# Graph attention with residual and layer norm: the queries' order read back earlier, the residual's bias summed on VectorE, the norm in single steps, q, k and v further ahead

## The chip, the cores and the metric

The kernel runs on one core of a Trainium2 chip, all in float32. The metric is the device time of one execution in microseconds. An engine is named as in the profile: PE is TensorE, DVE is VectorE, ACT is ScalarE, POOL is GpSimd (which also issues the gathers and scatters through DMA), SP is the queue that issues the plain DMAs. The five run side by side, each its own list of instructions in order, and wait for one another at semaphores.

## The reference

Sixteen graphs (b) of 1024 nodes (n) with 512 numbers each (d), 8 heads of 64; one adjacency matrix `adj` of 1024 x 1024 for all.

```python
q = (x @ Wq + bq).reshape(b, n, H, HD)          # k and v alike
scores = jnp.einsum('bqhd,bkhd->bhqk', q, k) / jnp.sqrt(jnp.float32(HD))
scores = scores + (1.0 - adj)[None, None, :, :] * -1000000000.0
attn = jax.nn.softmax(scores, axis=-1)
out = jnp.einsum('bhqk,bkhd->bqhd', attn, v).reshape(b, n, d)
return _layernorm(x + out @ Wo + bo)
```

The matrix is sparse and uneven: the first nodes have many neighbours, most have a few.

## The kernel before, in words

**Sparse attention by gathering.** The queries are sorted by their number of neighbours (`ranks`): eight tiles of 128 queries each. For tile t the kernel keeps lists (`edges`) of `OWN[t]` neighbours per query and, for the two tiles of the highest degree, `BLOCKS[t]` blocks of 128 further (query, neighbour) pairs. One block is 128 such pairs, one per partition: 29 own and 6 further ones, so 35 blocks in a batch and 560 in all. For a block POOL gathers rows of k and v (L809, tile kvg) and, once per tile or per further block, rows of q (L793 qt, L803 qg); DVE multiplies q by k (L826) and sums over each head (L830); ACT takes exponentials (L840); v is weighed by ACT (L850) or DVE (L854, `by_act` says which); own blocks are summed on DVE (L866), further ones with a matmul (L875, L876).

**The steps.** The loop over n at the end of the kernel writes the program out in one order for all engines: step n belongs to block n, with look-ahead (gathers 8 blocks ahead, products 4, exponentials 3). 34 steps of negative n lead in. `later(k, fn)` puts work k steps on into the middle of a step, `later_last` at its end. The simple jobs of the start (`loads`, `ranks`, `bias_setup`, `checks`, one `edges` per tile) are generators that run on to their next `yield` once a step; `EDGES_FROM[t]` is the step at which the lists of tile t begin. A list begins with a gather of 128 rows of `adj` in the sorted order (L412); three steps later the row is multiplied by the places 1 to 1024 (L417), and then DVE takes the eight largest at a time (L424, MAX8) and clears them (L426): ten rounds for the last tile, two for the one before, one for the others.

**The order of the queries.** `ranks` reads `adj` (8 tiles), sums its rows on ACT (L359), makes keys, turns them with PE (L369), counts on DVE how many keys are smaller (L376, eight passes over 1024), and scatters the queries to their places in DRAM with eight indirect DMAs of POOL (L384); SP reads the list back (L390) and DVE makes integers of it (L392, `asked_row`). No list, gather of q or store of a result can be issued before.

**q, k and v.** `pair(b, j)` makes q, k and v of two tiles of x with TensorE (L545, L661, with seven products of a fast 2x2 scheme for k and v); DVE and ACT take the sums out of PSUM, SP writes them to DRAM (`q_rows`, `kv_rows`, three batches in a ring). These units of TensorE work (`fronts`) run batches ahead of the attention. When all eight tiles of a batch are sent, a matmul makes the mean of v for queries without neighbours (L605) and SP writes it as the last row (L610); with that the batch counts as `set_up`, and DVE reduces its norms (L614). Gathers of a batch are issued only when it is set up.

**Which TensorE work in which step.** Each step gives TensorE a `share` in units (0.86 for a product of 128 x 512, 1.72 for two, 0.44 for four transposes); products of the output come first, then fronts. In the lead-in the share is 3.45. At the start of each batch it is set so that at its end the fronts are a fixed number of batches on (`goal`: the number of the batch plus 2, plus `EARLY / 35`). When the fronts have run out, some 50 steps before the end, ten attention tiles that were set aside in DRAM before (`SPILL`, the tiles 102 to 111) are finished beside the last ones, and the gathers go 11 ahead.

**The end of a tile.** When all blocks of a tile are in, it is normalised (L884 to L893), turned by PE (L901), and waits in `done`. `load_y` gathers the rows of x for the residual on POOL (L720); while there are fronts, and else for every odd t, POOL adds the bias `bo` to them two or three steps later (L726). `finish` makes the product with Wo, and DVE adds it to y and sums the row (L744; without POOL's bias L743 and L744). Then the norm: the mean in the next step (L749), squares on ACT at the end of the same step (L753), variance and its power -1/2 two steps on (L756 on DVE, L757 on POOL), the shift three steps on (L760), the result at the end of the fourth (L763), and the store two steps behind that, an indirect DMA of POOL (L767).

Of the kernel before, what the change touches and what calls it, by code (L numbers as in the profile page):

```python
# [14 lines left out]
OP = mybir.AluOpType  # L15
# [13 lines left out]
AHEAD = 8  # L29
KG_BUFS, QG_BUFS, QT_BUFS, PV_BUFS, Y_BUFS = 8, 4, 4, 5, 5  # L30
NO_ROW = 65536.0
# [6 lines left out]
ROWS = 3  # L38
EARLY = 11
LEAD_IN = 34  # L40
EDGES_FROM = (-14, -13, -12, -10, -8, -4, -6, -15)

# [110 lines left out]
def kernel(  # L153
# [66 lines left out]
    with ExitStack() as main:  # L220
# [125 lines left out]
        def ranks():  # L346
            for _ in range(2):
# [22 lines left out]
            yield  # L370
# [3 lines left out]
            yield  # L374
            for t in range(NT):
                nc.vector.scalar_tensor_tensor(  # L376
                    keys, row, key[:, t:t + 1], place, op0=OP.is_lt, op1=OP.min, accum_out=rank[:, t:t + 1]
                )
                if t % 3 == 2:
                    yield  # L380
            nc.vector.tensor_copy(rank_row, rank)
            yield
            for t in range(NT):
                nc.gpsimd.indirect_dma_start(  # L384
                    out=order_views[t], out_offset=bass.IndirectOffsetOnAxis(ap=rank_row[:, t:t + 1], axis=0),
                    in_=asked[:, t, :], in_offset=None,
                )
            for _ in range(2):
                yield
            nc.sync.dma_start(ranked, order.rearrange("(t p) c -> p t c", p=P))  # L390
            yield
            nc.vector.tensor_copy(asked_row, ranked[:, :, 0])  # L392
# [15 lines left out]
        def edges(t):  # L408
# [302 lines left out]

        loaded, biased = {}, {}

        def load_y(b, t, k=None):
            if k is None:
                Y[b, t] = work.tile([P, D], F32, tag="y", name=f"y_{b}_{t}", bufs=Y_BUFS)
            else:
                Y[b, t] = work.tile([P, 2, D], F32, tag=f"t{k % 4 + 1}", name=f"y_{b}_{t}", bufs=1)[:, 0, :]
            loaded[b, t] = now[0]
            nc.gpsimd.indirect_dma_start(  # L720
                out=Y[b, t], out_offset=None, in_=x_rows,
                in_offset=bass.IndirectOffsetOnAxis(ap=asked_row[:, t:t + 1], axis=0), element_offset=b * N * D,
            )

            if fronts or t % 2:
                later(2 if fronts else 3, lambda: nc.gpsimd.tensor_tensor(Y[b, t], Y[b, t], bo_bc, op=OP.add))  # L726
                biased[b, t] = True

# [6 lines left out]
        def finish(b, t):  # L735

            def out(p):
# [3 lines left out]
                st = small.tile([P, 5], F32, name="stats", bufs=6)  # L741
                if (b, t) not in biased:
                    nc.vector.tensor_tensor(y, p, y, op=OP.add)  # L743
                nc.vector.scalar_tensor_tensor(  # L744
                    y, p if (b, t) in biased else bo_bc, 1.0, y, op0=OP.mult, op1=OP.add, accum_out=st[:, 0:1]
                )

# [7 lines left out]
                def variance():  # L755
                    nc.vector.tensor_scalar(st[:, 2:3], st[:, 2:3], 1.0 / D, EPS, op0=OP.mult, op1=OP.add)  # L756
                    nc.gpsimd.tensor_tensor(st[:, 3:4], st[:, 2:3], neg_half, op=OP.pow)  # L757

# [28 lines left out]
        def gather(n):  # L787
            b, t, i = blocks[n]
            assert t in listed
            if i == 0:  # L790
                tag, bufs = ("qt", QT_BUFS) if fronts or t % 2 else ("x", 3)
                QT[b, t] = work.tile([P, D], F32, tag=tag, name=f"qt_{b}_{t}", bufs=bufs)
# [6 lines left out]
            else:  # L799
                g = first[t] + i - OWN[t]  # L800
                tag, bufs = ("qg", QG_BUFS) if fronts or i % 2 else ("xT", 4)
                QG[n] = work.tile([P, D], F32, tag=tag, name=f"qg_{n}", bufs=bufs)
# [39 lines left out]
        def by_act(n):  # L842
            b, t, i = blocks[n]
            return 0 < i < OWN[t] or n % 2 == 0

# [117 lines left out]
        prep.setdefault(12 - LEAD_IN, []).append(bias_setup())  # L963
        prep.setdefault(-24, []).append(checks())
        preps = [loads(), ranks()]
        prep.setdefault((B - 1) * NB - 4, []).append(guard())
        with tc.manual_schedule():
# [13 lines left out]
            while n < total or plan or rest or urgent or done or finishing or spilled:  # L981
# [105 lines left out]
```

## Time and profile before

| | |
|---|---|
| median of 3 runs | 2124.21 us (2122.94 to 2130.22) |
| the profiled execution | 2142.24 us |
| its span, first to last instruction | 2140.5 us |
| mean granted TensorE clock | 0.967 |
| busy: PE, DVE, ACT, POOL | 1946.7, 1810.1, 1686.2, 1474.0 us |

A row of a group names line, engine, operation, tiles (out<-in) and shapes, then the total busy time and the mean in ns of one, then the idle time of the engine before them and what ended it. A row of waits reads: engine, the instruction that waited, what it waited for, total us, number, longest. A row of the timeline: start, duration in us, engine, line. A row of windows: the stretch, its length, then busy us and instructions per engine, the granted TensorE clock, the busy share and the rate of the DMAs. "issue" is time in which an engine waited for nothing that the profile shows.

### The profile page before, as it was taken

How to read it: one execution, taken by the hardware profiler on the slowest of the kernel's cores; microseconds unless marked ns; L12 is line 12 of the kernel's file. 1: busy time of each engine (PE TensorE's matmuls, PEld its weight loads, DVE VectorE, ACT ScalarE, POOL GpSimd, SP SyncE). 2: the span in 40 equal slices, each digit the busy share in tenths (PEclk: the TensorE clock that was granted, in tenths of full speed). 3: DMA queues.
4: the chain of work that ended last, by engine and by line, in shares of the span. 5: the costliest groups of instructions: out<-in, count | busy, mean ns of one | idle time of the engine just before them, and what ended most of it. 6: DMA issues, size and time to landing. Idle time of an engine off the chain costs nothing. (4 is left out here: it accounts for less than half of the span.)

```text
span 2140.5 us, 26366 instructions
## 1 busy us (share of the span) xinstructions
PE 1946.7 (91%) x5334; PEld 930.5 (43%) x5334; DVE 1810.1 (85%) x3545; ACT 1686.2 (79%) x7024; POOL 1474.0 (69%) x1350
## 2 busy tenths in 40 slices
PE   8968999999999999999999999999999999998664
PEld 4423454444444444444444444444444444443222
DVE  2699999888988988798888878898889899997675
ACT  5526999788887988698797878888887889897575
POOL 1453778787776867667686766777677774668884
PEclk9988999999999999999999999999999999999887
DMA  6455888878787787878787786888878698978773
GB/s 251 133 182 182 276 277 282 298 252 293 237 283 241 266 305 240 281 230 283 257 280 277 246 279 203 285 282 268 293 241 308 223 317 306 318 229 305 220 233 107
DMA packets 183656, 549.49 MB, mean 257 GB/s; under 512 B 30879, under 2 KB 30907, under 8 KB 183486
## 3 DMA queue, kind: packets, MB, share of 16 engines
q0 software_dynamic: 121632, 403.22, 58.0%
q1 hardware_dynamic: 59248, 139.53, 17.4%
q10 hardware_dynamic: 2606, 4.99, 0.7%
q14 instruction: 126, 1.03, 0.1%
q8 instruction: 44, 0.72, 0.1%
HBM read 435.44 MB, written 136.89 MB: 267 GB/s over the span
## 5 line engine op out<-in xcount | busy, mean ns | idle before, releaser
L850 ACT ACTIVATE pv<-kvg,pv 128x64 f32<-128x64 f32 x3584 | 902.7, 339 | 1.6 <-remote 1.6
L809 POOL DMA_INDIRECT kvg<-kv_rows,key_row x560 | 638.0, 1139 | 306.5 <-issue 107.4
L545 PE MATMUL pq<-wq,xT 128*128 128x512 f32 x1024 | 483.3, 604 | 12.8 <-DVE q L572 11.2
L545 PE MATMUL po<-wo,oT 128*128 128x512 f32 x944 | 436.5, 602 | 6.3 <-ACT oT L905 3.4
L826 DVE TENSOR_TENSOR qk<-qt,kvg 128x512 f32<-128x512 f32 x464 | 355.6, 766 | 52.4 <-DMA kvg<-kv_rows,key_row 43.7
L830 DVE TENSOR_REDUCE s<-qk 128x8 f32<-128x512 f32 x560 | 380.7, 680 | 6.5
L545 PEld LDWEIGHTS pq<-wq,xT 128*128 128x128 f32 x1024 | 194.6, 194 | 244.8 <-issue 216.5
L545 PEld LDWEIGHTS po<-wo,oT 128*128 128x128 f32 x944 | 180.8, 194 | 227.6 <-issue 209.4
L840 ACT ACTIVATE pv<-s,absent 128x8 f32<-128x8 f32 x464 | 135.5, 293 | 150.5 <-DVE s L830 88.1
L661 PE MATMUL x<-b,xT 128*128 128x512 f32 x504 | 242.0, 603 | 3.3 <-ACT e L674 3.3
L866 DVE TENSOR_TENSOR pv<-pv,pv 128x520 f32<-128x520 f32 x336 | 242.6, 722 | 0.1
L661 PE MATMUL pp<-t,s 128*128 128x512 f32 x504 | 238.3, 595 | 1.1 <-DVE s L531 1.0
L753 ACT ACTIVATE ysq<-y,stats 128x512 f32<-128x512 f32 x128 | 91.9, 718 | 113.9 <-DVE stats L749 107.9
L726 POOL TENSOR_TENSOR y<-y,bo_bc 128x512 f32<-128x512 f32 x118 | 158.7, 1345 | 24.2 <-DMA y<-in_x_dram,asked_row 21.6
L793 POOL DMA_INDIRECT qt<-q_rows,asked_row x128 | 144.7, 1130 | 35.9 <-issue 35.0
L767 POOL DMA_INDIRECT out_dram<-y,asked_row x128 | 144.8, 1132 | 34.7 <-issue 22.1
L720 POOL DMA_INDIRECT y<-in_x_dram,asked_row x128 | 143.2, 1118 | 32.0 <-issue 31.7
L557 ACT ACTIVATE sq<-q 128x128 f32<-128x128 f32 x512 | 150.7, 299 | 13.7 <-DVE q L572 13.4
L757 POOL TENSOR_TENSOR stats<-stats,neg_half 128x1 f32<-128x1 f32 x128 | 83.4, 652 | 101.2 <-DVE stats L756 78.4
L557 ACT ACTIVATE sq<-kv 128x128 f32<-128x128 f32 x512 | 150.6, 299 | 0.0
L661 PEld LDWEIGHTS x<-b,xT 128*128 128x128 f32 x504 | 96.0, 193 | 118.7 <-issue 109.1
L661 PEld LDWEIGHTS pp<-t,s 128*128 128x128 f32 x504 | 95.0, 192 | 110.3 <-issue 101.9
(170 smaller groups left out, 2928.8 us busy)
## 6 DMA issues: line engine op xcount, KB each, us to landing
kv_rows<-kv SPq DMA_DIRECT2D x128, 512.0 KB
x<-in_x_dram SPq DMA_DIRECT2D x128, 256.0 KB
q_rows<-q SPq DMA_DIRECT2D x128, 256.0 KB
kvg<-kv_rows,key_row POOLq DMA_INDIRECT x560
adj<-in_adj_dram POOLq DMA_DIRECT2D x8, 512.0 KB
spill<-oT SPq DMA_DIRECT2D x10, 256.0 KB
oTs<-spill SPq DMA_DIRECT2D x10, 256.0 KB
qt<-q_rows,asked_row POOLq DMA_INDIRECT x128
```

The costliest lines, as they stand in the source:

```text
L545: nc.tensor.matmul(p, lhs()[:, ts(c, P)], w[:, c, :], start=(c == 0), stop=(c == NPAIR - 1))
L557: nc.scalar.activation(sq, s[:, ts(h, P)], AF.Square, accum_out=NRM[b][:, i, t, h:h + 1])
L661: nc.tensor.matmul(R[bank], l[:, ts(c, P)], right[:, c, :], start=(first and c == 0), stop=(c == 1), skip_group_check=True,)
L720: nc.gpsimd.indirect_dma_start(out=Y[b, t], out_offset=None, in_=x_rows, in_offset=bass.IndirectOffsetOnAxis(ap=asked_row[:, t:t + 1], axi ...
L726: later(2 if fronts else 3, lambda: nc.gpsimd.tensor_tensor(Y[b, t], Y[b, t], bo_bc, op=OP.add))
L767: nc.gpsimd.indirect_dma_start(out=out_rows[b, t], out_offset=bass.IndirectOffsetOnAxis(ap=asked_row[:, t:t + 1], axis=0), in_=y, in_offse ...
L793: nc.gpsimd.indirect_dma_start(out=QT[b, t], out_offset=None, in_=q_rows[b % ROWS], in_offset=bass.IndirectOffsetOnAxis(ap=asked_row[:, t: ...
L809: nc.gpsimd.indirect_dma_start(out=KG[n], out_offset=None, in_=kv_rows[b % ROWS], in_offset=bass.IndirectOffsetOnAxis(ap=key_row[:, g:g + ...
L826: nc.vector.tensor_tensor(QK[n], q, KG[n][:, 0:D], op=OP.mult)
L830: nc.vector.tensor_reduce(S[n], QK.pop(n).rearrange("p (h d) -> p h d", d=HD), axis=AX.X, op=OP.add)
L850: nc.scalar.activation(pv[:, ts(h, HD)], v[:, ds(D + h * HD, HD)], AF.Copy, scale=pv[:, D + h:D + h + 1])
L866: nc.vector.tensor_tensor(PV[b, t], PV[b, t], pv, op=OP.add)
```

## The change

Four things change, and some buffers with them.

1. *The order sooner.* `ranks` yields less often: the sums of three rows of `adj` per step instead of two, no step of its own for keys and copies, and each scatter is issued as soon as its rank is there, not all eight behind the last. The first use of the order moves from step -15 to step -20. `EDGES_FROM` begins most lists three steps sooner. The multiplication by place goes from POOL to DVE, and in the first 17 steps ACT alone weighs v.
2. *The bias on VectorE.* `load_y` no longer adds the bias; every tile takes the two instructions L743 and L744 that only few took. A product with Wo begins a step later after the load, five tiles of y may be loaded instead of four, and y has six buffers.
3. *The norm in steps.* Mean 1, squares 2, variance 3, power 4, shift 5, result 6 steps on; the store follows two steps behind as it did.
4. *q, k and v further ahead.* `EARLY` is 13 instead of 11, and in the goal of the first batch `FIRST`, 9, comes on top. The gathered q tiles of both kinds share seven buffers in place of four and four.

```diff
-KG_BUFS, QG_BUFS, QT_BUFS, PV_BUFS, Y_BUFS = 8, 4, 4, 5, 5
+KG_BUFS, Q_BUFS, PV_BUFS, Y_BUFS = 8, 7, 5, 6
-EARLY = 11
+EARLY = 13
+FIRST = 9
-EDGES_FROM = (-14, -13, -12, -10, -8, -4, -6, -15)
+EDGES_FROM = (-17, -16, -15, -13, -11, -8, -7, -18)
...
                 nc.scalar.activation(ADJ[t], ADJ[t], AF.Copy, accum_out=asked[:, t, 1:2])
-                if t % 2:
+                if t % 3 == 2:
                     yield
...
+                if t:
+                    nc.vector.tensor_copy(rank_row[:, t - 1:t], rank[:, t - 1:t])
+                    scatter(t - 1)
                 if t % 3 == 2:
                     yield
-            nc.vector.tensor_copy(rank_row, rank)
-            yield
-            for t in range(NT):
-                nc.gpsimd.indirect_dma_start(
...
-            nc.gpsimd.tensor_tensor(v, v, place, op=OP.mult)
+            nc.vector.tensor_tensor(v, v, place, op=OP.mult)
...
-            if fronts or t % 2:
-                later(2 if fronts else 3, lambda: nc.gpsimd.tensor_tensor(Y[b, t], Y[b, t], bo_bc, op=OP.add))
-                biased[b, t] = True
...
-                if (b, t) not in biased:
-                    nc.vector.tensor_tensor(y, p, y, op=OP.add)
-                nc.vector.scalar_tensor_tensor(
-                    y, p if (b, t) in biased else bo_bc, 1.0, y, op0=OP.mult, op1=OP.add, accum_out=st[:, 0:1]
-                )
+                nc.vector.tensor_tensor(y, p, y, op=OP.add)
+                nc.vector.scalar_tensor_tensor(y, bo_bc, 1.0, y, op0=OP.mult, op1=OP.add, accum_out=st[:, 0:1])
...
-                later_last(1, spread)
-                later(2, variance)
-                later(3, shift)
-                later_last(4, norm_out)
+                later_last(2, spread)
+                later(3, variance)
+                later(4, power)
+                later(5, shift)
+                later_last(6, norm_out)
...
-            return 0 < i < OWN[t] or n % 2 == 0
+            return 0 < i < OWN[t] or n % 2 == 0 or n < NB // 2
...
-        prep.setdefault(-24, []).append(checks())
+        prep.setdefault(-22, []).append(checks())
...
-                    goal = fronts_time - (n // NB + 2 + EARLY / NB) * batch_time
+                    goal = fronts_time - (n // NB + 2 + (EARLY + (FIRST if n < NB else 0)) / NB) * batch_time
...
-                    if tile_done not in loaded and sum(b * NT + t not in SPILL for b, t in Y) < 4:
+                    if tile_done not in loaded and sum(b * NT + t not in SPILL for b, t in Y) < 5:
...
-                    if not finishing and len(done) > (LAZY if fronts else 0) and n > loaded.get(done[0], n) and n > last_finish + 1:
+                    if not finishing and len(done) > (LAZY if fronts else 0) and n > loaded.get(done[0], n) + 1 and n > last_finish + 1:
```

The line numbers below are each kernel's own; behind L390 those of the changed kernel are larger by one to six where it has no line of the same number. On POOL, in the middle of the program, at the start of a batch: y_1 to y_3 are the residual rows of three tiles, kvg and qg gathers of the blocks, stats the norm's numbers. Before:

```order
L726 TENSOR_TENSOR y_1_10769<-y_1_10769,bo_bc 128x512
L720 DMA y_2_10848<-in_x_dram,asked_row 128x512
L803 DMA qg_10863<-q_rows_120,query_row 128x512
L809 DMA kvg_10865<-kv_rows_117,key_row 128x1024
L767 DMA out_dram<-y_7_10577,asked_row 16384x512
L793 DMA qt_7_10907<-q_rows_120,asked_row 128x512
L809 DMA kvg_10909<-kv_rows_117,key_row 128x1024
L726 TENSOR_TENSOR y_2_10848<-y_2_10848,bo_bc 128x512
```

And now:

```order
L725 DMA y_2_11020<-in_x_dram,asked_row 128x512
L810 DMA kvg_11032<-kv_rows_117,key_row 128x1024
L757 TENSOR_TENSOR stats<-stats,neg_half 128x1
L810 DMA kvg_11063<-kv_rows_117,key_row 128x1024
L810 DMA kvg_11098<-kv_rows_117,key_row 128x1024
L767 DMA out_dram<-y_7_10673,asked_row 16384x512
L725 DMA y_3_11135<-in_x_dram,asked_row 128x512
```

Between two gathers no sum over a whole tile is left; of arithmetic POOL keeps the power on one number per partition.

On DVE, where a batch is set up (gmax is the last instruction of that), qk products of the running batch still read a qg tile or an old qt, and those of the next batch read qt_0. Before, in the ninth batch:

```order
L614 TENSOR_REDUCE gmax<-nrm_10168 128x1 x2
L572 SCALAR_TENSOR_TENSOR q_0_11435<-pq_0_11397,bq_bc 128x512
L826 TENSOR_TENSOR qk_11457<-qg_11328,kvg_11330 128x512
L830 TENSOR_REDUCE s_11481<-qk_11457 128x8
L760 TENSOR_TENSOR stats<-stats 128x1
L680 TENSOR_TENSOR g_0_11485<-pp_9_0_11447,w_0_11408 128x512
L826 TENSOR_TENSOR qk_11523<-qt_0_11459,kvg_11461 128x512
```

And now:

```order
L619 TENSOR_REDUCE gmax<-nrm_10184 128x1 x2
L743 TENSOR_TENSOR y_4_11245<-po_4_11402,y_4_11245 128x512
L744 SCALAR_TENSOR_TENSOR y_4_11245,stats<-bo_bc,y_4_11245 128x512
L827 TENSOR_TENSOR qk_11440<-qg_11291,kvg_11293 128x512
...
L827 TENSOR_TENSOR qk_11482<-qg_11337,kvg_11339 128x512
...
L827 TENSOR_TENSOR qk_11539<-qg_11383,kvg_11385 128x512
...
L827 TENSOR_TENSOR qk_11567<-qt_0_11442,kvg_11444 128x512
```

One product of the old batch stood between the set-up and the first of the new; now there are three, and the bias of a tile y_4 stands on DVE.

On DVE in the lead-in, where the ranks are counted (keys, rank) and made integers for the scatters (rank_row). Before:

```order
L376 SCALAR_TENSOR_TENSOR keys,rank<-key_of,key,place 128x1024 x2
L381 CAST rank_row<-rank 128x8
L322 COPY bias_qk<-pb 128x8
L324 COPY bv_col<-pb 128x4
L326 COPY bvb<-bv_col 128x512
```

And now:

```order
L383 SCALAR_TENSOR_TENSOR keys,rank<-key_of,key,place 128x1024 x2
L387 CAST rank_row<-rank 128x1
L383 SCALAR_TENSOR_TENSOR keys,rank<-key_of,key,place 128x1024
L387 CAST rank_row<-rank 128x1
L577 SCALAR_TENSOR_TENSOR q_2_360<-pq_2_323,bq_bc 128x512
```

The scatters no longer wait for the last of the eight passes, and the passes stand ahead of the third q tile instead of beside the bias set-up.

More of the change, by code (lines that the diff above doesn't have):

```diff
@@ L346, in ranks @@
         def ranks():
-            for _ in range(2):
-                yield
+            yield
             for t in range(NT):
@@ L374, in ranks, with scatter @@
             yield
+            def scatter(t):
+                nc.gpsimd.indirect_dma_start(
+                    out=order_views[t], out_offset=bass.IndirectOffsetOnAxis(ap=rank_row[:, t:t + 1], axis=0),
+                    in_=asked[:, t, :], in_offset=None,
+                )
             for t in range(NT):
@@ L378, in ranks @@
                 )
+                if t:
+                    nc.vector.tensor_copy(rank_row[:, t - 1:t], rank[:, t - 1:t])
+                    scatter(t - 1)
                 if t % 3 == 2:
                     yield
-            nc.vector.tensor_copy(rank_row, rank)
+            nc.vector.tensor_copy(rank_row[:, NT - 1:NT], rank[:, NT - 1:NT])
+            scatter(NT - 1)
             yield
-            for t in range(NT):
-                nc.gpsimd.indirect_dma_start(
-                    out=order_views[t], out_offset=bass.IndirectOffsetOnAxis(ap=rank_row[:, t:t + 1], axis=0),
-                    in_=asked[:, t, :], in_offset=None,
-                )
-            for _ in range(2):
-                yield
             nc.sync.dma_start(ranked, order.rearrange("(t p) c -> p t c", p=P))
+            yield
             yield
@@ L710, in pair @@
             return units
-        loaded, biased = {}, {}
+        loaded = {}
         def load_y(b, t, k=None):
@@ L756, in variance, with power @@
                     nc.vector.tensor_scalar(st[:, 2:3], st[:, 2:3], 1.0 / D, EPS, op0=OP.mult, op1=OP.add)
+                def power():
                     nc.gpsimd.tensor_tensor(st[:, 3:4], st[:, 2:3], neg_half, op=OP.pow)
@@ L790, in gather @@
             if i == 0:
-                tag, bufs = ("qt", QT_BUFS) if fronts or t % 2 else ("x", 3)
+                tag, bufs = ("qt", Q_BUFS) if fronts or t % 2 else ("x", 3)
                 QT[b, t] = work.tile([P, D], F32, tag=tag, name=f"qt_{b}_{t}", bufs=bufs)
@@ L800, in gather @@
                 g = first[t] + i - OWN[t]
-                tag, bufs = ("qg", QG_BUFS) if fronts or i % 2 else ("xT", 4)
+                tag, bufs = ("qt", Q_BUFS) if fronts or i % 2 else ("xT", 4)
                 QG[n] = work.tile([P, D], F32, tag=tag, name=f"qg_{n}", bufs=bufs)
```

2 lines of the change are left out of this document (removed).

## The prediction

> **What bounds the kernel now.** I read the page first, then the busy times stage by stage, then who waits for whom, and last the timeline where a wait stood out. The page says how much TensorE there is:
>
> ```profile
> PE 1946.7 (91%) x5334; PEld 930.5 (43%) x5334; DVE 1810.1 (85%) x3545; ACT 1686.2 (79%) x7024; POOL 1474.0 (69%) x1350
> ```
>
> No edit takes a matmul away, so the time can fall only by what is left of the span, 2140.5 - 1946.7 = 194 us of idle TensorE (and a little where its clock was low). The windows say where that idle time is. I cut them at the score reductions (L830, one per step), whose first stands here:
>
> ```profile
> 141.66 0.69 DVE L830 TENSOR_REDUCE s<-qk 128x8 f32<-128x512 f32 x1
> ```
>
> ```profile
> core 0: us, PE busy (x) PEld busy (x) DVE busy (x) ACT busy (x) POOL busy (x), PEclk, DMA share, GB/s
> 0.00:141.70 141.70, 120.92 (x316) 55.58 (x316) 84.32 (x142) 64.19 (x212) 54.10 (x60) 0.98 0.54 184
> 141.70:279.30 137.60, 114.21 (x311) 54.41 (x312) 130.82 (x269) 100.17 (x438) 83.34 (x73) 0.91 0.71 236
> 279.30:392.80 113.50, 107.96 (x309) 52.06 (x307) 102.86 (x202) 101.23 (x426) 88.81 (x81) 1.00 0.84 281
> 392.80:1757.20 1364.40, 1307.33 (x3624) 628.03 (x3625) 1189.85 (x2322) 1134.22 (x4787) 989.09 (x889) 0.98 0.79 267
> 1757.20:1860.80 103.60, 97.82 (x282) 47.53 (x280) 97.37 (x175) 94.93 (x432) 57.70 (x50) 0.98 0.89 303
> 1860.80:1930.00 69.20, 64.73 (x184) 31.00 (x184) 64.27 (x123) 57.75 (x245) 46.87 (x44) 1.00 0.79 263
> 1930.00:2100.00 170.00, 116.89 (x273) 53.31 (x272) 122.99 (x276) 116.78 (x433) 139.26 (x142) 0.85 0.76 248
> 2100.00:2140.50 40.50, 16.86 (x43) 8.56 (x41) 17.59 (x44) 16.95 (x55) 14.83 (x16) 0.79 0.18 68
> ```
>
> Call them the lead-in, batch 0, batch 1, the middle (11 batches of 35 steps, 124.0 us each), the batch that sets tiles aside, a piece before the tail, the tail, the end. Three limits alternate. Batch 0 is VectorE's: 130.8 of 137.6. The middle is TensorE's: 1307 of 1364, 57 idle. The tail is GpSimd's: its 139.3 us are 82%, but its queue stood for nothing else than its own issuing, as its waits there show (the first is of that kind, the second the longest of another):
>
> ```profile
> POOL kvg L809 <- issue: 13.0, 44, 0.5
> ...
> POOL y L726 <- DMA y<-in_x_dram,asked_row: 1.2, 1, 1.2
> ```
>
> In the middle, TensorE's longest wait, and VectorE's three longest:
>
> ```profile
> PE pxT L516 <- DVE y L744: 27.5, 10, 4.7
> ```
>
> ```profile
> DVE y L744 <- POOL y L726: 52.6, 24, 4.2
> DVE qk L826 <- DMA kvg<-kv_rows,key_row: 38.8, 8, 7.3
> DVE stats L760 <- POOL stats L757: 17.5, 14, 3.4
> ```
>
> So nearly half of TensorE's idle time there is a transpose behind L744, and L744 waits for the bias sum on GpSimd. The second row is the change of batch:
>
> ```profile
> 626.23 0.24 SPq L610 DMA_DIRECT2D kv_rows<-mean  x1
> ```
>
> ```profile
> 630.13 0.68 DVE L680 TENSOR_TENSOR g<-pp,w 128x512 f32<-128x512 f32 x1
> 637.51 0.69 DVE L826 TENSOR_TENSOR qk<-qt,kvg 128x512 f32<-128x512 f32 x1 [6.70 <-issue]
> ```
>
> The next batch's last row is written at 626.2, its first product runs at 637.5, and VectorE stands 6.7 us in between, since only one old product was left to do.
>
> **The bias on VectorE.** Beside the waits the GpSimd sum costs VectorE time that counts as busy. A product that overlaps it, and what the groups say of this:
>
> ```profile
> 1964.11 1.27 POOL L726 TENSOR_TENSOR y<-y,bo_bc 128x512 f32<-128x512 f32 x1
> ```
>
> ```profile
> 1963.61 2.33 DVE L826 TENSOR_TENSOR qk<-qt,kvg 128x512 f32<-128x512 f32 x1
> ```
>
> ```profile
> L830 DVE TENSOR_REDUCE s<-qk 128x8 f32<-128x512 f32 x560 | 380.7, 680 | 6.5
> L826 DVE TENSOR_TENSOR qk<-qt,kvg 128x512 f32<-128x512 f32 x464 | 355.6, 766 | 52.4 <-DMA kvg<-kv_rows,key_row 43.7 <-issue 8.4
> L744 DVE SCALAR_TENSOR_TENSOR y<-po,y 128x512 f32<-128x512 f32 x118 | 80.7, 684 | 72.5 <-POOL y L726 62.8 <-PEq L1057 6.9 <-PE po L545 2.7
> L760 DVE TENSOR_TENSOR stats<-stats 128x1 f32<-128x1 f32 x128 | 40.6, 317 | 61.7 <-POOL stats L757 46.1 <-issue 15.4
> L749 DVE TENSOR_SCALAR stats<-stats 128x1 f32<-128x1 f32 x128 | 18.4, 144 | 0.0
> L743 DVE TENSOR_TENSOR y<-po,y 128x512 f32<-128x512 f32 x10 | 6.8, 677 | 0.0
> ```
>
> The product took 2.33 us instead of some 0.68 and ended only after the sum did. Against equal-sized neighbours L826 is long by 464 x 0.086 = 40 us and L760 by 128 x 0.173 = 22 us: 62 us of VectorE that are really waiting. The edit adds 118 sums out of PSUM at 0.677 (L743's row, the same instruction): 80 us. It returns the 62 us and the wait of 62.8 us. VectorE gains some 45 us; GpSimd loses 158.7 us of work.
>
> Does VectorE keep a second burden? GpSimd's small power reads SBUF too and stays:
>
> ```profile
> 1976.51 0.72 POOL L757 TENSOR_TENSOR stats<-stats,neg_half 128x1 f32<-128x1 f32 x1
> ```
>
> ```profile
> 1976.12 0.69 DVE L866 TENSOR_TENSOR pv<-pv,pv 128x520 f32<-128x520 f32 x1
> ```
>
> The sum of two SBUF tiles beside it kept its 0.69 us, so I charge nothing. The Trainium skill (SBUF — State Buffer, "Who interferes with whom") says otherwise: a VectorE instruction with two SBUF inputs contends with any GpSimd instruction that reads SBUF, and one holds the other for its whole length. For the bias sum this trace agrees (2.33 us); for the power it does not. By the rule the power would hold VectorE again; that is a rival below.
>
> **Further ahead.** By the planner's own units a batch of q, k, v is 4 x (7 x 1.72 + 8 x 0.86 + 0.88) = 79.2 us. At the end of batch 0 it now wants 2 + 22/35 batches done instead of 2 + 11/35: 25 us more matmuls in batch 0. In batch 1 it wants 3 + 13/35, so 20 us less than the full batch it asked for before. From then on two steps' worth more: set-up comes two steps sooner, three old products stand where one stood (order rows above). Three steps of 124.0 / 35 = 3.5 us are 10.6; the chain took 637.5 - 626.2 = 11.3. The wait of the second row falls to about 1 us per batch. One buffer fewer for q (7 for 4 + 4) costs nothing: a q tile lives at most the 8 steps of look-ahead and its own blocks, and a query block's tile is taken again only after seven others.
>
> **The middle.** 27.5 us go with the bias. The other 29.6 us of idle TensorE are small waits for VectorE; with 38.8 + 17.5 us of its waits nearly gone, I take 12 of them: 39 us. What is late next are VectorE's weighing and normalising; 18 us of idle stay. Ends: 15 (the waits find new causes) and 57.
>
> **Lead-in and batch 0.** The order is known when asked_row is written, and the lists start from it:
>
> ```profile
> 88.81 0.17 DVE L392 CAST asked_row<-ranked 128x8 int32<-128x8 f32 x1 [5.46 <-DMA ranked<-order]
> ...
> 99.48 1.22 DVE L424 MAX8 kl<-codes 128x8 f32<-128x1024 f32 x1
> ...
> 138.27 3.35 DVE L826 TENSOR_TENSOR qk<-qt,kvg 128x512 f32<-128x512 f32 x1
> ```
>
> From 99.5 on VectorE is nearly full up to 279. The lists now start three steps sooner, 3 x 3.45 = 10 us by the planner's share. The eight multiplications by place come to VectorE at about the 1.22 us of a pass over 1024 (9.8 us); GpSimd's went over products like the 3.35 us one (2.7 too long), and three blocks' weighing goes to ScalarE (100 of 137.6 us there). GpSimd's queue changes too: the order's scatters now stand ahead of all eight clears of the adjacency tiles, and the lists' reads between them, so that a read waits for ScalarE's check; no row prices that. I set these against each other at 0, ends +10 and -8. Batch 0 then needs 114.2 + 25 = 139 us of TensorE, some 142 with its small waits: 4 more than now. Sum -6, ends +6 and -16.
>
> **Batch 1.** TensorE falls to 108 - 20 = 88 us and VectorE becomes the limit. The nearest row is the one from 1757.2: a whole batch of q, k, v without a layer norm, 103.6 us with VectorE at 97.4 and ScalarE at 94.9. Batch 1 has a quarter less of that and eight layer norms more; I take 104.5: -9, ends -3 and -12.
>
> **Tail and end.** Here every GpSimd instruction counts:
>
> ```profile
> 1930.00:2100.00 170.00, 14.20 (x11) 0.85 0.76 248
> ```
>
> Those are the bias sums in the tail: 14.2 us, less about 0.1 us each for the longer gap between two DMA issues: -13. VectorE has room there (123 of 170). The last tile's chain has one more sum of 0.68: +1. The norm's further steps and the later start of a product (one step more after the load) hide behind other tiles until the last two; the steps behind the last block hold no other work, so they are short. Together -12, ends -6 and -16. The other two stages: 0.
>
> **The sum.** -6 - 9 - 39 - 12 = -66 us, so a span near 2074.5. The profiled execution took 2142.24 us for its span of 2140.5, 18 us over the median of the runs; I take the same difference off the median: 2124.2 - 66 = 2058. The ends give -18 to -101, thus 2106 to 2023.
>
> **The rivals.**
> - *The waits only move* (0.15). TensorE keeps its 57 us in the middle because VectorE, at 87% there, still comes late. Then -27: 2097. Against it: one cause holds 27.5 us by name.
> - *TensorE runs nearly through* (0.10). With the waits its low clock goes too (0.98 in the middle: some 26 us). Then 57 and half of the 26 there: 2027.
> - *The power holds VectorE*, by the SBUF rule (0.03). In the middle 88 of them, each holding a product for the 0.72 us of its row, would add 63 us to 1190, still under TensorE's 1307; I let them eat half the gain there: 2077.
> - *VectorE becomes the bound: slower* (0.06). If L826 and L760 are long for a reason that stays, the middle's VectorE grows by 88 x 0.677 = 60 to 1250, with its 56 us of the other two waits 1306: level with TensorE, so that waits no longer hide. I put that at +10 there, +14 in batch 0 (4 above, 10 of multiplications), and 0 elsewhere: 2148. It decides when VectorE's busy time per batch passes 118 us. The 2.33 us row speaks against it.
> - That the earlier order brings nothing, since lists and products share VectorE: 2064, inside the forecast.
>
> **How the numbers follow.** 0.66 is left for the forecast. 0.3% (6.4 us) is what a measurement here can tell. Faster by more: nearly all of 0.66 + 0.15 + 0.10 + 0.03, less a little for small gains: 0.91. Within: 0.03. Slower: 0.06. The range from 2028 to 2104 leaves out the slow case, half of the fastest and the edges.
>
> **What would show it.** Right: no product over 0.8 us in L826's group (mean near 0.68), L760 near 0.15; no wait for GpSimd's bias; the middle at 120 to 121 us per batch; batch 1 near 104 with VectorE over 95%; GpSimd still back to back in the tail, 13 us shorter. Wrong: VectorE's busy time above 1860, TensorE's idle time in the middle above 45, or batch 0 above 150.

## The result, and the profile after

The changed kernel takes 2044.98 us (median of 4 runs, 2043.34 to 2046.64), the kernel before 2123.57 us in the same runs: ratio 0.9626, 95% interval 0.9602 to 0.965, some 79 us less. The forecast was 2058, the range 2028 to 2104. The profiled execution took 2043.34 us for a span of 2041.5. The page's first part, and the windows of the changed kernel cut at the same score reductions (lead-in, batch 0, batch 1, the 11 batches of the middle, everything behind them):

```profile
PE 1917.2 (94%) x5334; PEld 925.4 (45%) x5334; DVE 1801.0 (88%) x3675; ACT 1684.6 (83%) x7048; POOL 1302.5 (64%) x1224
```

```profile
0.00:140.30 140.30, 123.20 (x313) 56.78 (x314) 92.18 (x173) 64.02 (x212) 41.68 (x56) 0.96 0.57 189
140.30:281.30 141.00, 130.40 (x360) 61.85 (x359) 124.45 (x266) 110.16 (x490) 69.45 (x65) 0.96 0.73 246
281.30:389.30 108.00, 97.65 (x275) 46.55 (x273) 99.42 (x203) 96.75 (x403) 71.85 (x70) 0.98 0.81 268
389.30:1671.70 1282.40, 1278.17 (x3616) 621.03 (x3617) 1186.66 (x2407) 1128.45 (x4792) 874.33 (x802) 1.00 0.83 285
1671.70:2041.50 369.80, 287.75 (x773) 139.17 (x771) 298.24 (x629) 285.25 (x1154) 245.19 (x234) 0.91 0.76 255
```

The middle is where the time went: 1282 us for 1364, 116.6 per batch, and TensorE is idle for 4 us of it where it was idle for 57. What is left there of its waits and of VectorE's (the longest of each), and the groups that the prediction named, stand here:

```profile
PE pxT L521 <- DVE q L577: 2.2, 1, 2.2
PE poT L902 <- ACT xT L525: 1.2, 1, 1.2
```

```profile
DVE stats L754 <- ACT ysq L751: 20.5, 19, 3.5
DVE y L743 <- PE po L550: 10.9, 10, 2.0
...
DVE stats L760 <- POOL stats L757: 5.6, 6, 1.4
DVE qk L827 <- DMA kvg<-kv_rows,key_row: 4.0, 5, 2.0
```

```profile
L827 DVE TENSOR_TENSOR qk<-qt,kvg 128x512 f32<-128x512 f32 x464 | 317.4, 684 | 5.9 <-DMA kvg<-kv_rows,key_row 5.8
L867 DVE TENSOR_TENSOR pv<-pv,pv 128x520 f32<-128x520 f32 x336 | 233.1, 694 | 0.2 <-ACT pv L851 0.2
L760 DVE TENSOR_TENSOR stats<-stats 128x1 f32<-128x1 f32 x128 | 19.3, 151 | 41.5 <-POOL stats L757 41.5
L422 DVE TENSOR_TENSOR codes<-codes,place 128x1024 f32<-128x1024 f32 x8 | 9.8, 1221 | 0.0
```

VectorE's waits for GpSimd's bias (52.6 us) are gone, those for a gather at the change of batch fell from 38.8 to 4.0, and VectorE now waits for ScalarE's squares (L754: 20.5 us; the same wait was 5.4 in the profile before) and for TensorE (L743) instead. A product takes 0.684 us where it took 0.766. The spread of single ones comes from the view of one line (shortest, median, longest in ns):

```profile
L827 DVE TENSOR_TENSOR qk<-qt,kvg x464: 669/682/759, 139.6 to 1995.2; 128x512 f32<-128x512 f32 x155
```

### The profile page after: what moved, and what is told of

The parts are those of the page before. It is cut to its first block, busy times and chain, and to the rows that moved or that the text cites. A ratio compares the mean times of both kernels' runs of the same rounds, so it can differ in the third digit from the quotient of the medians.

```text
span 2041.5 us, 26505 instructions
## 1 busy us (share of the span) xinstructions
PE 1917.2 (94%) x5334; PEld 925.4 (45%) x5334; DVE 1801.0 (88%) x3675; ACT 1684.6 (83%) x7048; POOL 1302.5 (64%) x1224
## 5 line engine op out<-in xcount | busy, mean ns | idle before, releaser
L827 DVE TENSOR_TENSOR qk<-qt,kvg 128x512 f32<-128x512 f32 x464 | 317.4, 684 | 5.9 <-DMA kvg<-kv_rows,key_row 5.8
L550 PEld LDWEIGHTS po<-wo,oT 128*128 128x128 f32 x944 | 176.5, 192 | 209.2 <-issue 191.8
L867 DVE TENSOR_TENSOR pv<-pv,pv 128x520 f32<-128x520 f32 x336 | 233.1, 694 | 0.2 <-ACT pv L851 0.2
L767 POOL DMA_INDIRECT out_dram<-y,asked_row x128 | 151.0, 1180 | 35.5 <-issue 16.9
L794 POOL DMA_INDIRECT qt<-q_rows,asked_row x128 | 140.4, 1097 | 38.9 <-issue 34.6
L666 PEld LDWEIGHTS x<-b,xT 128*128 128x128 f32 x504 | 95.8, 191 | 116.6 <-issue 111.5
L902 PE MATMUL poT<-ident,o 128*128 128x128 f32 x512 | 79.5, 279 | 50.2 <-DVE o L894 34.1
L666 PE MATMUL z<-b,s 128*128 128x512 f32 x252 | 120.1, 599 | 5.0 <-DVE kv L694 5.0
L804 POOL DMA_INDIRECT qg<-q_rows,query_row x96 | 106.9, 1114 | 27.8 <-issue 24.1
```

The costliest lines, as they stand in the source:

```text
L550: nc.tensor.matmul(p, lhs()[:, ts(c, P)], w[:, c, :], start=(c == 0), stop=(c == NPAIR - 1))
L666: nc.tensor.matmul(R[bank], l[:, ts(c, P)], right[:, c, :], start=(first and c == 0), stop=(c == 1), skip_group_check=True,)
L767: nc.gpsimd.indirect_dma_start(out=out_rows[b, t], out_offset=bass.IndirectOffsetOnAxis(ap=asked_row[:, t:t + 1], axis=0), in_=y, in_offse ...
L794: nc.gpsimd.indirect_dma_start(out=QT[b, t], out_offset=None, in_=q_rows[b % ROWS], in_offset=bass.IndirectOffsetOnAxis(ap=asked_row[:, t: ...
L827: nc.vector.tensor_tensor(QK[n], q, KG[n][:, 0:D], op=OP.mult)
L867: nc.vector.tensor_tensor(PV[b, t], PV[b, t], pv, op=OP.add)
```

## The experiments

The theory going in (A): the bias sum on GpSimd cost most of it, as a wait and as VectorE instructions held up beside it. The rival (B): the distance of q, k and v did it. Later a third question came up, what FIRST and the earlier order are each worth. Each run is told by its ratio to the kernel before on its own chip; on the chip of a_first0, a_early11, a_norm and a_order the kernel before took 2139 us, on the others 2124 to 2126.

**b_control**: the kernel before, once more.

> The kernel before, unchanged, for a second profile. Its time is that of before, 2123 us. The profile shown of before took 2142 us, 18 us over the median. If those 18 us are a whim of that one execution, this profile is near 2123 and its middle (1364.4 us there) near 1346, so that the change won some 64 us in the middle and not 82. If instead profiles always run longer than other executions, this one is near 2142 again.

Its span is 2123.4 us, ratio 1.0015 (0.9998 to 1.0032). Its middle, and TensorE's longest wait and VectorE's three longest in it:

```profile
397.50:1740.40 1342.90, 1296.93 (x3629) 624.36 (x3628) 1196.06 (x2323) 1134.59 (x4793) 987.17 (x890) 0.99 0.80 272
```

```profile
PE pxT L516 <- DVE y L744: 27.2, 10, 4.7
```

```profile
DVE y L744 <- POOL y L726: 52.9, 24, 4.2
DVE qk L826 <- DMA kvg<-kv_rows,key_row: 41.8, 10, 6.5
DVE stats L760 <- POOL stats L757: 22.6, 18, 3.5
```

So the 18 us by which the profile shown of before stood over the median lay in the middle, and were that execution's own: TensorE's idle time there is 46 us, not 57. The change won 60 us in the middle (1342.9 to 1282.4), not 82. Below, the middle is compared with this one.

**b_bias**: the kernel before with the bias on VectorE alone.

```diff
-            if fronts or t % 2:
-                later(2 if fronts else 3, lambda: nc.gpsimd.tensor_tensor(Y[b, t], Y[b, t], bo_bc, op=OP.add))
-                biased[b, t] = True
...
-                if (b, t) not in biased:
-                    nc.vector.tensor_tensor(y, p, y, op=OP.add)
-                nc.vector.scalar_tensor_tensor(
-                    y, p if (b, t) in biased else bo_bc, 1.0, y, op0=OP.mult, op1=OP.add, accum_out=st[:, 0:1]
-                )
+                nc.vector.tensor_tensor(y, p, y, op=OP.add)
+                nc.vector.scalar_tensor_tensor(y, bo_bc, 1.0, y, op0=OP.mult, op1=OP.add, accum_out=st[:, 0:1])
```

> The kernel before with one thing changed: every tile takes its bias on VectorE, GpSimd has no sum. Theory A (the bias sum cost most of what was won: as a wait for GpSimd and as VectorE instructions held up beside it): the middle falls by 30 to 45 us, the tail by some 12, 2066 to 2082 us in all; L826 near 0.68 us and L760 near 0.15; the wait at the change of batch (38.8 us on VectorE) stays. Theory B (the distance of q, k and v did most, the bias little): 2100 to 2115 us.

2054.74 us, ratio 0.9659 (0.9628 to 0.969): 70 us from this part alone, more than theory A asked for. Products take 0.697 us and L753 (the same instruction as L760) 0.151, as theory A had it. Its middle, and the waits that stay:

```profile
386.90:1680.20 1293.30, 1282.10 (x3620) 620.96 (x3621) 1183.61 (x2409) 1131.27 (x4791) 859.80 (x802) 1.00 0.82 282
```

```profile
DVE qk L819 <- DMA kvg<-kv_rows,key_row: 34.4, 11, 6.5
DVE stats L749 <- ACT ysq L746: 24.9, 17, 3.2
DVE stats L753 <- POOL stats L750: 16.6, 11, 5.4
```

The two pages give the size of what was held up. The first line is b_control's, the second b_bias's:

```profile
PE 1943.0 (91%) x5334; PEld 928.9 (44%) x5334; DVE 1819.7 (86%) x3545; ACT 1684.8 (79%) x7024; POOL 1468.8 (69%) x1350
```

```profile
PE 1924.4 (94%) x5334; PEld 925.1 (45%) x5334; DVE 1800.8 (88%) x3663; ACT 1680.7 (82%) x7024; POOL 1308.2 (64%) x1232
```

VectorE does 118 instructions more, 118 x 0.682 = 80 us, and is yet 19 us less busy: 99 us of its busy time beside GpSimd's sums had been waiting, 0.84 us per sum.

**a_poolbias**: the changed kernel with the sum on GpSimd again, by the lines removed in b_bias.

> The changed kernel with its bias back on GpSimd (two or three steps after the load, for the same tiles as before). Theory A: it loses what b_bias gains, 40 to 55 us, so 2085 to 2100 us, with products again over 0.8 us. Theory B: it keeps most of the gain, 2055 to 2065 us.

2079.61 us, ratio 0.9786 (0.9758 to 0.9814), between the two theories. Products take 0.774 us again, and VectorE's busy time is 1833.8 us with 117 instructions fewer, so 33 + 117 x 0.684 = 113 us are held up. But the wait for the bias is 10.2 us in the whole run (62.4 in b_control), in a program that loads five tiles of y instead of four and begins the product a step later: the wait could be taken away with the sum still on GpSimd, the holding was not. What grows is the wait for GpSimd's power, from 5.6 to 33.1 us in the middle. Its middle:

```profile
394.70:1698.10 1303.40, 1285.05 (x3623) 621.22 (x3624) 1216.25 (x2320) 1131.80 (x4793) 1000.77 (x891) 1.00 0.83 280
```

Bias alone wins 70 us, all other parts without it 45, both together 79 to 83: they don't add up. Two reliefs of one shortage would behave so (VectorE comes late, and either less work or fewer waits on it helps); that reading is argued here, not tested by itself.

**a_dummy**: the changed kernel with an idle sum.

```diff
+            if b and (fronts or t % 2):
+                later(2 if fronts else 3, lambda: nc.gpsimd.tensor_tensor(place[:, D:], bo_bc, place[:, :D], op=OP.add))
```

> The changed kernel with a sum of the same size added on GpSimd where the bias sum stood, from batch 1 on; it reads two tiles that nobody writes any more and its result is read by nobody, so nothing waits for it. It parts the two costs of the bias sum. If holding up VectorE is real, L827 grows to about 0.76 us and VectorE's busy time by 50 to 60 us; in the middle VectorE then has 1187 + 50 = 1240 us, still under TensorE's 1278, so that the time there grows by 5 to 20 us, and the tail by 12 for GpSimd's queue: 2060 to 2077. If only the wait counted and the long products were a coincidence, L827 stays at 0.68 us and only the tail grows: 2050 to 2058.

2116.32 us, ratio 0.9962 (0.9942 to 0.9981): some 3.5% over the changed kernel, almost the whole gain lost, and far over what was expected. Nothing waits for these 109 sums. The first line of the page, the middle, and one sum with the product beside it, from the timeline:

```profile
PE 1941.2 (92%) x5334; PEld 928.5 (44%) x5334; DVE 1921.1 (91%) x3675; ACT 1693.3 (80%) x7048; POOL 1454.4 (69%) x1333
```

```profile
397.10:1734.40 1337.30, 1294.07 (x3616) 621.14 (x3617) 1285.47 (x2407) 1135.36 (x4790) 995.65 (x892) 0.99 0.81 273
```

```profile
438.72 1.27 POOL L730 TENSOR_TENSOR place<-bo_bc,place 128x512 f32<-128x512 f32 x1
```

```profile
438.57 1.98 DVE L829 TENSOR_TENSOR qk<-qt,kvg 128x512 f32<-128x512 f32 x1
```

The same 3675 instructions of VectorE take 120 us more, 1.1 us per sum. In the middle VectorE is then busy 1285 of 1337 us, 96%: it has become the bound, and TensorE stands 43 us. The waits for the power, behind the sums in GpSimd's queue, are 6.3 us there, hardly more than the 5.6 of the changed kernel, so it is the holding that costs the middle. Which instructions are held, by their groups:

```profile
L829 DVE TENSOR_TENSOR qk<-qt,kvg 128x512 f32<-128x512 f32 x464 | 368.6, 794 | 8.8 <-DMA kvg<-kv_rows,key_row 8.7
L746 DVE SCALAR_TENSOR_TENSOR y<-bo_bc,y 128x512 f32<-128x512 f32 x128 | 111.4, 870 | 4.4
L833 DVE TENSOR_REDUCE s<-qk 128x8 f32<-128x512 f32 x560 | 380.4, 679 | 6.4
L745 DVE TENSOR_TENSOR y<-po,y 128x512 f32<-128x512 f32 x128 | 87.2, 681 | 14.4 <-PE po L550 14.4
```

Those that read two tiles of SBUF have grown, products from 0.684 us and L746 from 0.695. Score reductions, which read one, and L745, which reads one tile of SBUF and one of PSUM, have not. Where the expectation failed: it charged VectorE with 50 to 60 us, and the products did grow by 51; but the other groups that read two SBUF tiles grew by some 70 us besides. And it took 1240 us of VectorE under 1278 of TensorE as nearly free; at 1285 it was not.

**a_dummy_one**: the same with one tile read instead of two.

```diff
-                later(2 if fronts else 3, lambda: nc.gpsimd.tensor_tensor(place[:, D:], bo_bc, place[:, :D], op=OP.add))
+                later(2 if fronts else 3, lambda: nc.gpsimd.tensor_scalar(place[:, D:], bo_bc, 1.0, None, op0=OP.add))
```

> The changed kernel with the idle GpSimd instruction of a_dummy, but reading one tile instead of two (a constant added to it). If GpSimd's second SBUF input is what holds VectorE, L827 stays at 0.68 us and the time within 12 us of the changed kernel (the queue's 11 instructions in the tail). If any instruction of GpSimd over 128x512 holds VectorE, it is like a_dummy: VectorE busier by some 100 us, 50 to 70 us slower than the changed kernel.

2098.33 us, ratio 0.9867 (0.9852 to 0.9882), 55 us over the changed kernel on the same chip. Neither expectation fits. The instruction itself, and VectorE's waits in the middle:

```profile
L730 POOL TENSOR_SCALAR place<-bo_bc 128x512 f32<-128x512 f32 x109 | 183.7, 1685 | 2.5
```

```profile
DVE stats L762 <- POOL stats L759: 54.4, 24, 3.6
DVE qk L829 <- DMA kvg<-kv_rows,key_row: 14.2, 11, 2.9
```

VectorE's busy time grows by 38 us only (1838.5), and products take 0.708 us. What the trace shows besides is the queue: each instruction takes 1.685 us of GpSimd, and the powers behind it come late (54.4 us of VectorE's waits in the middle against 4.4 in a_again). How the 55 us divide between the two was not parted by an experiment. A comparison gives an idea: a_poolbias has VectorE as busy in the middle (1216.3 us, here 1215.0) and 33.1 us of waits for the power instead of 54.4, and its middle is 1303.4 us, here 1315.9.

**a_first0, a_first0_again and a_again**: q, k, v in the first batch as in the others; and the changed kernel once more, on the chip of the second.

```diff
-FIRST = 9
+FIRST = 0
```

> The changed kernel with FIRST at 0: 9/35 of a batch of q, k, v (some 20 us of TensorE) less in batch 0, handed on to batch 1. If batch 0 is only filled to TensorE's limit by FIRST and batch 1 gets it back (theory of the prediction: +4 and -9), batch 0 falls from 141 to about 134 us, batch 1 rises from 108 to about 114, the sum moves by 0 to +5 us: 2045 to 2050. Rival: FIRST only moved the load about, 2041 to 2047.

> The changed kernel with FIRST at 0, once more, beside the changed kernel on one chip. Theory C, from the last profiles: the earlier order is worth 18 us in batch 0 (137.7 us before, 119.9 with FIRST 0), and FIRST spends 21 of it on TensorE work that batch 1 returns only 3 of, since batch 1 has no engine that is full. Then this is 13 to 20 us faster than the changed kernel. Rival: the ratio 0.948 was the chip's, and the two differ by under 6 us.

> The changed kernel once more, beside the next three on one chip, since the chip of the last four gave 2139 us for the kernel before where the others gave 2124. Ratio to before 0.963 as measured already; if the chips differ in more than a factor, 0.955 to 0.970.

a_first0 has a ratio of 0.9478 (0.9453 to 0.9503), a_first0_again 0.9507 (0.9494 to 0.952), a_again 0.9611 (0.9598 to 0.9625). Without FIRST the kernel is 21 us faster, 2022.15 against 2043.05 us on one chip: the fastest version here. The first expectation failed, the second (theory C) held but for one microsecond, and that of a_again held. Batches 0 and 1 of a_again, then of a_first0_again:

```profile
138.60:276.20 137.60, 128.48 (x360) 60.51 (x359) 124.18 (x265) 110.28 (x490) 68.14 (x65) 0.98 0.75 252
276.20:384.30 108.10, 98.70 (x275) 47.70 (x274) 99.47 (x204) 97.81 (x408) 71.97 (x70) 0.97 0.82 269
```

```profile
140.40:260.30 119.90, 112.80 (x315) 54.02 (x314) 117.21 (x254) 104.11 (x459) 68.99 (x62) 0.96 0.80 267
260.30:371.20 110.90, 110.52 (x318) 53.96 (x317) 105.11 (x215) 102.27 (x433) 76.19 (x72) 1.00 0.84 284
```

FIRST puts 16 us of matmuls into a batch where TensorE has 7 us of room and VectorE 3; that batch grows by 18 us. The next batch loses 12 us of matmuls and gets 3 us shorter: VectorE's work there falls by 6 only.

**a_early11**: FIRST 0, and EARLY 11 as before.

```diff
-EARLY = 13
+EARLY = 11
-FIRST = 9
+FIRST = 0
```

> The changed kernel with q, k, v as far ahead as before (EARLY 11, FIRST 0). The old distance leaves one product of the old batch behind the set-up, and b_bias, which has it, still shows 34.4 us of VectorE waiting for gathers there against 4.0 in the changed kernel. If that wait reaches the end, the middle grows by some 11 us (b_bias has 1293 against 1282): 2053 to 2060. Rival: VectorE has room for it once the bias sums no longer hold it up, and the time stays at 2043 to 2049.

Ratio 0.9573 (0.9546 to 0.9599), to be compared with a_first0 on the same chip, 0.9478: the two steps of EARLY are worth 19 us, more than the 11 expected; 13 of them are in the middle of these two profiles. The expected time, 2053 to 2060, was missed (2045.4), since FIRST at 0 was not reckoned as a gain; by its ratio the run would take 2033 us where before takes 2124. The rival failed too, as the wait did come back. The middles of a_early11 and of a_first0, and the longest wait of VectorE in a_early11's:

```profile
372.00:1668.50 1296.50, 1282.10 (x3620) 621.18 (x3621) 1185.43 (x2411) 1126.59 (x4786) 852.86 (x800) 1.00 0.83 281
```

```profile
371.10:1654.60 1283.50, 1279.93 (x3624) 621.12 (x3623) 1185.53 (x2406) 1126.86 (x4783) 877.25 (x802) 1.00 0.84 285
```

```profile
DVE qk L827 <- DMA kvg<-kv_rows,key_row: 27.4, 16, 4.5
```

**a_norm and a_norm_again**: the norm's steps of before, with the variance and the power in one step.

```diff
-                later_last(2, spread)
-                later(3, variance)
-                later(4, power)
-                later(5, shift)
-                later_last(6, norm_out)
+                later_last(1, spread)
+                later(2, variance)
+                later(3, shift)
+                later_last(4, norm_out)
```

> The changed kernel with the layer norm in the steps of before (1, 2, 2, 3, 4). The prediction charged the longer chain with nothing: 2042 to 2048. Rival: single steps took VectorE's waits for ScalarE and GpSimd away (24.9 and 16.6 us in b_bias's middle against 20.5 and 5.6), and without them it is 2050 to 2058.

> The changed kernel with the norm's steps of before, once more, beside the changed kernel on one chip. By the prediction within 6 us of it. If single steps are worth something: 8 to 15 us slower, with VectorE waiting for GpSimd's power (22.5 us in the middle against 5.6).

Ratios 0.9651 (0.9624 to 0.9678) and 0.9664 (0.9651 to 0.9678); on the chip of the second 2056.22 us against 2043.05. So single steps are worth 13 us, where the prediction put nothing, and the rival held. The middle of a_norm_again and VectorE's waits in it:

```profile
393.00:1683.00 1290.00, 1279.81 (x3620) 621.33 (x3620) 1183.91 (x2406) 1129.98 (x4794) 875.90 (x803) 1.00 0.83 283
```

```profile
DVE stats L759 <- POOL stats L756: 28.8, 16, 3.6
DVE stats L754 <- ACT ysq L751: 25.9, 21, 2.2
DVE qk L825 <- DMA kvg<-kv_rows,key_row: 17.2, 18, 2.8
```

The waits for the power are 28.8 us, against 4.4 in a_again, and those for gathers 17.2 against 3.1. The middle is 7 us longer than a_again's 1283.1; the rest lies in the stages around it. It is not worth that everywhere: a_early11, with single steps, has no shorter middle than b_bias without them (1296.5 and 1293.3, on two chips).

**a_order**: the order, the lists' starts, the multiplication by place and the weighing as before, all else changed. In the main:

```diff
-EDGES_FROM = (-17, -16, -15, -13, -11, -8, -7, -18)
+EDGES_FROM = (-14, -13, -12, -10, -8, -4, -6, -15)
...
-            nc.vector.tensor_tensor(v, v, place, op=OP.mult)
+            nc.gpsimd.tensor_tensor(v, v, place, op=OP.mult)
...
-            return 0 < i < OWN[t] or n % 2 == 0 or n < NB // 2
+            return 0 < i < OWN[t] or n % 2 == 0
```

> The changed kernel with the queries' order, the lists' starts, the multiplication by place (on GpSimd) and the weighing of the first steps as before. The prediction set the parts of this against each other at 0, ends +10 and -8, since lists and products share VectorE: 2041 to 2049, the end of batch 1 near 389 us. Rival: the earlier order is what lets batch 0 take the extra matmuls; without it batch 0 grows by 6 to 12 us: 2051 to 2057.

Ratio 0.9654 (0.9628 to 0.9681), 0.3 to 0.4% over the changed kernel's two ratios, which were measured on other chips; so the answer rests on the stages. Lead-in and batch 0:

```profile
0.00:143.30 143.30, 123.62 (x316) 56.51 (x316) 84.28 (x141) 64.20 (x212) 54.16 (x60) 0.96 0.52 182
143.30:291.80 148.50, 127.25 (x356) 60.64 (x357) 136.82 (x286) 104.81 (x466) 76.99 (x69) 0.95 0.72 237
```

VectorE does 84 us in the lead-in and 137 in batch 0; with the earlier order 92 and 124. So 8 us of work on the lists moved to where VectorE stood idle, and 5 us are gone altogether; which of the four parts saves these was not parted. The end of batch 0 comes at 281.3 or 276.2 us instead of 291.8: worth some 10 to 15 us there, of which 6 to 9 are left at the end by the ratios. On a_order's own chip only a_norm can be set beside it, with the order early but the norm as before: its batch 0 ends at 284.9, 7 us sooner. By the stages the rival held: batch 0 is 8 to 11 us longer, 4 beside a_norm.

## Why the prediction was right, and where it was not

*The bias* (right in kind, too small). Both costs of the sum on GpSimd were named, and both are real: a_dummy shows the holding up without the wait, and the 52.9 us of waiting in b_control's middle are gone in b_bias. The step that failed in size is "62 us of VectorE that are really waiting": 99 were. Only two groups had been compared with their neighbours; L866 (0.732 to 0.694), L854 and others were held up as well. No product is longer than 0.76 us now, as the prediction asked for, and L760 takes 0.151.

*The middle* (mis-sized: -39 forecast, -60 measured against b_control and -82 against the profile that the prediction read). "18 us of idle stay" was wrong, 4 do: the small waits for VectorE went with the large one; with the bias alone (b_bias) 11 stay. TensorE's busy time fell too, from 1297 to 1278, as its granted clock went from 0.99 to 1.00. That is the rival "TensorE runs nearly through", which had 0.10, and was right for this stage. The row of 27.5 us that the argument leaned on is best read as one symptom of a VectorE that came late everywhere.

*The change of batch* (right): the wait falls from 41.8 to 4.0 us, and a_early11 shows it come back. By that run EARLY is worth 19 us, 13 of them in the middle, which the prediction had inside its 12 for small waits.

*Lead-in and batch 0* (right sum by luck, two wrong terms). Forecast -6; measured +2 against the profile of before, and -4.4 and, in a_again, -9.5 against b_control. But the earlier order, taken as 0 with ends +10 and -8, is worth some 10 us there (7 to 15 by the comparisons above), and FIRST, taken as 4 us, costs 18 in batch 0, though TensorE has 130.4 us of work there and not 139. They cancelled. "From 99.5 on VectorE is nearly full" was a right reading: it is busy for 41.0 of the 42.2 us up to the first score reduction. The step that failed is what was made of it. Before 99.5 VectorE is busy for only 43.3 us, and the lists that start three steps sooner put work there (52.6 us in the changed kernel), where it displaces no products. The two windows of before, then the first of the changed kernel:

```profile
0.00:99.50 99.50, 87.83 (x240) 41.60 (x241) 43.30 (x76) 56.48 (x175) 30.02 (x44) 1.00 0.55 193
99.50:141.70 42.20, 33.09 (x77) 13.97 (x75) 41.02 (x68) 7.71 (x37) 24.08 (x16) 0.92 0.51 162
```

```profile
0.00:99.50 99.50, 90.29 (x242) 42.85 (x242) 52.62 (x96) 56.31 (x175) 29.08 (x44) 0.98 0.60 204
```

With that batch 0 would have been 120 us long (a_first0_again), and filling it with matmuls to 140 was no longer hidden.

*Batch 1* (sign right, mis-sized): -9 forecast, to 104.5; it is 108.0 and 108.1, -5.5 against the profile of before and -3.8 against b_control. "VectorE becomes the limit" failed: it is at 92% and not over 95%, and no engine is full there. TensorE has 97.7 us of work in it and not 108 - 20 = 88. What else holds the batch up stays open.

*The norm's steps* (wrong): charged with nothing, worth 13 us. "Hide behind other tiles" looked only at the length of the chain and not at the engines' queues: with variance and power in one step, VectorE's next instruction of the norm comes up before GpSimd is done (28.8 us of such waits), and all that is queued behind it on VectorE waits too. The longer distance and the single steps came in one edit, so which of the two does it was not parted.

*Tail and end* (right in the sum only): from the end of the middle on 383.3 us before, 369.8 and 371.7 now (a_again), -12 as forecast. But only part of that is in the tail and the end: counted from the same score reduction, the 48th from the last, they fall from 207.7 to 201.2 us (203.3 in a_again), and the rest lies in the two stages that the prediction put at 0. The bias is a cause: with it alone (b_bias) the stretch behind the batch that sets tiles aside falls from 279.4 (b_control) to 270.0, and a_poolbias, a_dummy and a_dummy_one, with the instructions back on GpSimd, need 278.7, 282.7 and 284.5 us there against the changed kernel's 268.6 and 270.5. That it is GpSimd's queue fits a_dummy_one, which is the longest though it holds VectorE least; these runs do not part the two.

*VectorE becomes the bound* did not happen (1186.7 us in the middle, 108 per batch), but a_dummy brought it about: at 1285.5 / 11 = 117 us per batch, next to the 118 named as the point from which it decides.

*The power holds VectorE* did not happen: with 128 powers left, L827's mean is 0.684 us. The rule that suggested it (the Trainium skill, "SBUF — State Buffer", section "Who interferes with whom": a VectorE instruction with two SBUF inputs contends with a GpSimd instruction that reads SBUF) agrees with a_dummy, where VectorE lost 1.1 us for each sum of 1.31. It does not agree with the power, and only in part with a_dummy_one (38 us lost over 109 instructions).

## What to carry to other kernels

A row of waits shows where lateness came out, not all that it cost: to price a relief, take the busy time that the cause adds in every group, not in the one with the largest mean. And an engine that serves three others can cost time before it is full: here VectorE at 93% of the middle, with waits for GpSimd beside it, cost 21 us (a_poolbias). Work moved early is free only where the stage it goes to has room on the engine that bounds it after the other edits, and worth something only if the stage it leaves is bound by it: here a gain of the earlier order was spent on FIRST, and leaving FIRST out made the kernel 21 us faster still. A chain of small instructions through several engines can be worth spreading over more steps of the program, as long as other tiles fill them: here it brought 13 us, though it made the chain longer.

## What the runs showed of the hardware that was not expected

A sum of two SBUF tiles on GpSimd holds VectorE's instructions with two SBUF inputs for about its own length, 1.1 us of 1.31 on average over 109 sums (a_dummy), though nothing depends on it. The power, with one number per partition in each operand, held no product visibly: its 128 instructions are still there in the changed kernel, and the longest product takes 0.759 us. An instruction of GpSimd over the same 128x512 with one input holds them far less, 38 us in all, though it takes longer itself (1.685 us). Of 47 products that began during it 36 kept their length, like the one shown; those already running lost some 0.3 us at the median.

```profile
354.36 1.51 POOL L730 TENSOR_SCALAR place<-bo_bc 128x512 f32<-128x512 f32 x1
```

```profile
354.86 0.68 DVE L829 TENSOR_TENSOR qk<-qt,kvg 128x512 f32<-128x512 f32 x1
```

Why that is so was not tried. The same kernel before took 2139 us on one chip and 2124 to 2126 on the others, so that ratios and times of one chip are the safe comparison.
